# Turning tiles in 32 by 32 blocks on VectorE and placing the blocks by DMA, in an attention and FFN kernel

## The chip, the core and the metric

The kernel runs on one core of one Trainium2 chip. The core has TensorE (PE: matrix products, and transposes as products with an identity), VectorE (DVE), ScalarE (ACT), GpSimd (POOL), and the queue of SyncE (SP), from which most DMAs are issued. Sixteen DMA engines serve all queues. The metric is the time on the device in microseconds (us), the median of several runs.

## The reference

The input is x of 4 batches, 1024 rows and 512 columns, in float32. What is computed:

```python
def attn(x, Wqkv, bqkv, Wo, bo):            # 16 heads of 32
    kqv = (x @ Wqkv + bqkv).reshape(b, s, 3, 16, 32)
    q, k, v = kqv[:, :, 0], kqv[:, :, 1], kqv[:, :, 2]
    scores = jnp.einsum('bsnh,btnh->bnst', k, q) / math.sqrt(32)
    scores = jnp.triu(scores) + -10000.0 * jnp.tril(ones, k=-1)
    a = jax.nn.softmax(scores, axis=2)
    return jnp.einsum('bnkq,bknh->bqnh', a, v).reshape(b, s, 512) @ Wo + bo

def ffn(y, ...):                            # int32 weights, 2048 wide
    W = (wq.astype(float32) - 128) * scale[:, None]     # for gate, up, down
    return (silu(y @ Wg.T) * (y @ Wu.T)) @ Wd.T

x = x + layernorm(attn(layernorm(x)))
x = x + layernorm(ffn(layernorm(x)))
```

Both layer norms ahead of products are of interest here: the normalized rows lie with rows in partitions, and the products need them with columns in partitions, so each tile of 128 rows by 512 columns must be turned. v, which the projection makes with its columns in partitions, must be turned the other way.

## The kernel before

**Attention.** Work goes by batch b (4), by head block hb (4 blocks of 4 heads), and by half g of the 1024 columns. A pair (b, hb) takes 12 periods: 4 for g = 0, then 8 for g = 1, one for each tile c of 128 keys. A period p does, for its tile, the products of scores to be exponentiated (`weights`, L346: PE into PSUM, ACT's exponential at L384, a triangle on POOL at L386), for a later pair the products whose maxima are wanted (`maxima`, L261: PE, then a minimum and a reduction on DVE, L288 and L292), and the products with v of the tile before (`values`, L395). Each period has two halves u. There are 192 periods after 12 that lead in. In this document the position of a period is p modulo 12; a period begins in the trace with the first of four L359 products. In the first periods of g = 1 the sums over keys are made by accumulating DMAs that POOL issues (L434, two of 512 KB a period): these are issued at the start of the periods at positions 6 to 9. The last two pairs of hb and g go without.

**What goes between.** A planner written in Python places the other work (L655 to L860). Three lanes hold projection pieces with a cost and a due period (`in_piece`, `project_out`); four lists hold whole pieces: "rows", "ln", "turn" and "scan". In its first half each period takes at most one whole piece (`fill_whole`, L770); if none was there, it may take a projection piece at this place (`fill`, L756), and at the end of the period more of them. The order is fixed when the kernel is built; every engine runs its own instructions in that order, SP too.

Three things matter here:
- `ln_stage` (L669) is a pipeline over the eight row tiles of a batch: load (L494), statistics (L76, L77, L79, L80), normalize (L86, DVE), turn. `ln_turn` (L505) makes four PE transposes into one PSUM bank, and ACT copies the bank to `xnT` (L515). For batch 0 this runs before the first period; for the others it is spread over the periods of the batch before.
- `turn_v` (L536) turns half of v of a pair: four PE transposes (L543) and an ACT copy (L544) into `vt`, which `values` reads from the pair's first period on.
- `look` (L583) reads all weights once, to see whether a split into two fp32r parts is exact: 48 tiles, three in four periods from period 0 on, each a DMA on SP (L581) and a maximum on DVE at the period's end (L585). Two buffers: after a look the load for the look after next can start.

`store_out` (L572) and `project_out` (L553) make the output rows of the attention and keep them in DRAM (`x2`), through loads and stores on SP.

**FFN.** Eight groups of four row tiles; each group has 16 iterations i of `gate_up` (L966) and `down` (L998), 24 products in an iteration. While a group runs, the next is prepared: rows loaded at i = 5, means at 7, tile k normalized (`layernorm_tile`, L941) at i = 8 + k and turned (`layernorm_turn`, L956) at i = 9 + k: four PE transposes into a bank of the gate and up products (L960), a cast on ACT (L962), a difference on DVE (L964). The first group is prepared during the attention by `ffn_stage` (L618), in the same manner. Weight blocks are loaded and converted by `load_blocks` (L908) in the even iterations of the first group. In the FFN SP's order is left to the scheduler of the framework.

Of the kernel before, what the change touches and what calls it, by code (L numbers as in the profile page):

```python
# [10 lines left out]
F32 = mybir.dt.float32  # L11
F32R = mybir.dt.float32r
BF16 = mybir.dt.bfloat16
I32 = mybir.dt.int32
# [4 lines left out]
P = 128  # L19
# [8 lines left out]
def tile_attn_ffn_sandwich(  # L28
# [15 lines left out]
    nc = tc.nc  # L44
    B, S, H = x.shape
    I = gate_wt.shape[1]
    HC = H // P
    D = 32
    HPB = P // D
    NJ = S // P  # L50
    NT = B * NJ
    IC = I // P
    GT = 4
# [6 lines left out]
    dram = ctx.enter_context(  # L60
        tc.tile_pool(name="between", bufs=1, space=bass.MemoryType.DRAM)
    )
    x2 = dram.tile([B, S, H], F32, tag="x2", name="x2")
    ident = keep.tile([P, P], F32, tag="ident", name="ident")
    make_identity(nc, ident)

# [18 lines left out]
    def normalized(dst, src, mv, i):  # L85
        nc.vector.tensor_scalar(  # L86
            dst, src, mv[:, i, 0:1], mv[:, i, 1:2], ALU.subtract, ALU.mult
        )

    def weight_blocks(k):  # L90

# [7 lines left out]
    with ExitStack() as actx:  # L99
# [9 lines left out]
        e1, e2, e3, p4 = right("a_e1", 1), right("a_e2", 2), right("a_e3", 3), right("a_4", 4)  # L109
        cpool = right("a_w", 1)  # L110
        p1, p2, p3 = right("a_1", 1), right("a_2", 2), right("a_3", 3)
# [80 lines left out]
        for g, t in enumerate(least):  # L192
# [21 lines left out]

        actx.enter_context(
            tc.manual_schedule(
                engines={
# [16 lines left out]
        state = {}  # L236
        later = []

        def beside(shape, name, dtype=F32):

            first = state.get("first", False) and not state.get("last")
            state["first"] = False
            pool, tag = (ps_own, "own") if first else (ps_big, "big")
            return pool.tile(shape, dtype, tag=tag, name=name)
# [253 lines left out]
        def ln_norm(b, j):  # L500
            xn = e2.tile([P, H], F32, tag="xn", name=f"xn_{b}_{j}")
            normalized(xn, state.pop(("xr", b, j)), state.pop(("mv", b, j)), 0)
            state["xn", b, j] = xn

        def ln_turn(b, j):  # L505
            half, i = divmod(j, NJ // 2)
            if i == 0:
                state["xnT", b, half] = pxn.tile(
                    [P, HC, S // 2], F32, tag="xnT", name=f"xnT_{b}_{half}"
                )  # L510
            xn = state.pop(("xn", b, j))
            pt = beside([P, HC, P], f"xt_{b}_{j}")
            for c in range(HC):
                nc.tensor.transpose(pt[:, c, :], xn[:, ts(c, P)], ident)
            nc.scalar.copy(state["xnT", b, half][:, :, ts(i, P)], pt)  # L515
# [20 lines left out]
        def turn_v(b, hb, half):  # L536

            if half == 0:
                state["vt", b, hb] = p2.tile([P, NJ, P], F32, tag="vt", name=f"vt_{b}_{hb}")
            vT = state["v", b, hb]  # L540
            pv = beside([P, 4, P], f"pv_{b}_{hb}_{half}")
            for i in range(4):
                nc.tensor.transpose(pv[:, i, :], vT[:, ts(4 * half + i, P)], ident)  # L543
            nc.scalar.copy(state["vt", b, hb][:, 4 * half : 4 * half + 4, :], pv)  # L544

        def later_v(b, hb):

# [29 lines left out]

        def look_load(n):
            if n < len(blocks):
                state["look", n] = e2.tile([P, 512], I32, tag="look", name=f"look_{n}")  # L580
                nc.sync.dma_start(state["look", n], blocks[n])  # L581

        def look(n):  # L583
# [73 lines left out]
        emitted = {}  # L657
# [7 lines left out]
        def in_piece(b, hb, which, q):  # L665
            project(b, hb, which, q)
            count(("v" if which == 2 else "qk", b, hb))

        def ln_stage(b, j):  # L669

            if j < NJ:
                ln_load(b, j)
            if 0 <= j - 1 < NJ:
                ln_stats(b, j - 1)
            if 0 <= j - 2 < NJ:
                ln_norm(b, j - 2)
            if 0 <= j - 3 < NJ:
                ln_turn(b, j - 3)
            count(("ln", b))

        def normed(b, q):
            return emitted.get(("ln", b), 0) >= NJ // 2 * (q // 2 + 1) + 3

        def turn_piece(b, hb, half):
            turn_v(b, hb, half)
# [4 lines left out]
        NQ = S // 256  # L690
        for b in range(B):
            here, after = at[b, 0, 0], at[b, 0, 0] + n_periods // B
            for j in range(NJ + 3):

                put(whole["ln"], 0, here - 24,
                    lambda p, b=b, j=j, t=here - 46: p >= t and (
                        j - 3 < NJ // 2 or b == 0 or emitted.get(("v", b - 1, HC - 1), 0) >= 2
                    ),
                    ln_stage, b, j)
            for hb in range(HC):  # L700
                i = at[b, hb, 0]
                for q in range(NQ):
                    for which in range(2):

                        put(lanes["qk"], FULL, i - LEAD - 1 + (4 if q >= NQ // 2 else 0),
                            lambda p, b=b, i=i, q=q: p >= i - 24 and normed(b, q),
                            in_piece, b, hb, which, q)

                early = 2 if (b, hb) == (B - 1, HC - 1) else 0
                for q in range(NQ):  # L710
                    put(lanes["v"], FULL, i - 4 - 2 * early,
                        lambda p, b=b, i=i - early, q=q: p >= i - 11 and normed(b, q),
                        in_piece, b, hb, 2, q)
                for half in range(2):
                    put(whole["turn"], 0, i - 2,

                        lambda p, b=b, hb=hb, half=half, n=NQ // 2 * (half + 1):
                            emitted.get(("v", b, hb), 0) >= n
                            and (not half or at[b, hb, 0] == 0
                                 or ("shared", steps[steps.index((b, hb, 0)) - 1]) in emitted),  # L720
                        turn_piece, b, hb, half)
            for j in range(NJ):
                for half in range(2):
                    due = after + 39
                    put(lanes["out"], FULL, min(due, n_periods - 1 if j < 4 else n_periods + 9),
                        lambda p, t=after - 4 + WAIT if j < 4 else after + 4 + WAIT: p >= t,
                        project_out, b, j, half)
            put(lanes["out"], 0.1, due + 1,
                lambda p, b=b: state.get(("rows at", b, NJ - 1), p) < p, store_out, b, NJ - 1)

        def heads(of, p):
            return sorted(
                (lane[0][1], k) for k, lane in of.items() if lane and lane[0][2](p)
            )
# [33 lines left out]
                most -= 1  # L768

        def fill_whole(p):  # L770
            ahead = sorted(heads(whole, p), key=lambda h: h[1] not in ("rows", "scan"))
            if ahead:
                piece(whole[ahead[0][1]])
            return bool(ahead)


        while emitted.get(("ln", 0)) != NJ + 3:
# [20 lines left out]
        for p in range(-LEAD, n_periods + 1):  # L798
# [52 lines left out]
            if p >= 0 and p % 4 != 3:  # L851
                n = next(looks, None)
# [22 lines left out]
    def ffn(exact):  # L875
        MM = F32R if exact else F32
        with ExitStack() as fctx:
# [18 lines left out]
            p2 = pool("f_2", 2)  # L896
            p4 = pool("f_4", 4)
            spool = pool("f_stage", 3)
            e1 = pool("f_e", 1)
            ps_acc = pool("f_acc", 1, space=bass.MemoryType.PSUM)  # L900
            ps_gu = pool("f_gu", 4, space=bass.MemoryType.PSUM)
# [23 lines left out]
            rows, means, xns, normed = {}, {}, {}, {}  # L925
# [15 lines left out]
            def layernorm_tile(t0, i):  # L941
                if i == 0:
                    if exact and t0 // GT % 2 == 0:
                        normed[t0] = [pre["hi"], pre["lo"]]
                    else:
                        normed[t0] = [
                            (p1 if exact else p2).tile(
                                [P, HC, GT * P], MM, tag=f"xnT2{k}", name=f"xnT2{k}_{t0}"
                            )
                            for k in range(1 + exact)  # L950
                        ]
                xn = p2.tile([P, H], F32, tag="xn2", name=f"xn2_{t0 + i}")
                normalized(xn, rows[t0][i], *means[t0 + i])
                xns[t0 + i] = xn

            def layernorm_turn(t0, i):  # L956
                xn = xns.pop(t0 + i)
                pt = ps_gu.tile([P, HC, P], F32, tag="gu", name=f"xt2_{t0 + i}")
                for c in range(HC):
                    nc.tensor.transpose(pt[:, c, :], xn[:, ts(c, P)], ident)  # L960
                parts = [t[:, :, ts(i, P)] for t in normed[t0]]
                nc.scalar.copy(parts[0], pt)  # L962
                if exact:
                    nc.vector.tensor_tensor(parts[1], pt, parts[0], ALU.subtract)  # L964
# [79 lines left out]
            kept = []  # L1044
            for t0 in range(0, NT, GT):
                for i in range(IC):
# [4 lines left out]
                    was, nxt = t0 - GT, t0 + GT  # L1051
# [6 lines left out]
                        load_rows(nxt)  # L1058
                    if nxt < NT and i == 7:
                        layernorm_means(nxt, range(GT))  # L1060
                    if nxt < NT and 0 <= i - 9 < GT:
                        layernorm_turn(nxt, i - 9)
                    if nxt < NT and 0 <= i - 8 < GT:
                        layernorm_tile(nxt, i - 8)
                    if len(kept) > 1 and (nxt < NT or i < IC - 2):
# [65 lines left out]
```

## Time and profile before

| What | us |
|---|---|
| median of 3 runs (range) | 1895.65 (1895.38 to 1896.06) |
| the profiled execution | 1899.55 |
| its span, first to last instruction | 1897.8 |
| PE busy | 1827.5 |
| DVE busy | 1170.4 |
| POOL busy | 720.0 |
| ACT busy | 662.5 |
| four PE transposes of v, from their start to the next product | 0.58 |
| an FFN iteration with a turn, without | 5.94, 5.44 |

The attention with its lead-in takes up to about 1180 us, the FFN the rest. Times in the lines that follow are from the span's start. A line of a group gives line, engine, operation, output and input names, shapes and count, then busy us and mean ns of one, then the idle time of the engine before them and what ended it. A line of a timeline gives start and length. A window line gives, for each engine, busy us and the number of instructions, and at the end the clock granted to TensorE as a share, the busy share of the DMA engines and GB/s. A line of the DMA view gives the packets of a queue, MB, and the share of the 16 engines' time; or a kind of DMA with its count, size and the median us from issue to landing.

### The profile page before, as it was taken

The numbers are of one execution on the slowest core, as the hardware profiler recorded it, in microseconds if no ns is written. First come the engines' busy times: TensorE is split into PE (matmuls) and PEld (weight loads), VectorE is DVE, ScalarE is ACT, GpSimd is POOL, SyncE is SP. The second block draws the span as 40 slices with busy tenths as digits, with TensorE's granted clock in tenths as the row PEclk, the third lists the DMA queues.
The fourth block names the chain that finished last, engine by engine and source line by source line (L and its number), as shares of the span: only waits on it lengthen the run. The fifth ranks groups of instructions, "written<-read, shape, count | busy, mean of one in ns | idle before, by whom it ended". The sixth has DMA issues, their size and how long they took to land. (4 is left out here: it accounts for less than half of the span.)

```text
span 1897.8 us, 40784 instructions
## 1 busy us (share of the span) xinstructions
PE 1827.5 (96%) x17760; PEld 1079.7 (57%) x17761; DVE 1170.4 (62%) x1817; ACT 662.5 (35%) x994; POOL 720.0 (38%) x1000
## 2 busy tenths in 40 slices
PE   7899999999999999999999889999999999999997
PEld 4333444444444444444444335888888888888886
DVE  4688887787776687776667755544444444444344
ACT  2244444444424444424444341222222222222221
POOL 2165555465575465565555653001101010101011
PEclk9999999999999999999999999999999999999999
DMA  3164346435335325424414613501010000101000
GB/s 115 59 145 111 88 110 129 109 78 118 74 80 112 68 63 101 96 63 90 90 37 114 148 68 106 172 34 45 6 40 23 23 17 28 45 1 45 1 23 24
DMA packets 65627, 137.48 MB, mean 72 GB/s; under 512 B 6304, under 2 KB 20640, under 8 KB 65440
## 3 DMA queue, kind: packets, MB, share of 16 engines
q0 software_dynamic: 17280, 62.92, 18.0%
q1 hardware_dynamic: 41008, 67.40, 10.6%
q10 hardware_dynamic: 7152, 4.46, 0.8%
q8 instruction: 141, 2.31, 0.5%
q14 instruction: 46, 0.38, 0.1%
HBM read 55.07 MB, written 16.78 MB: 38 GB/s over the span
## 5 line engine op out<-in xcount | busy, mean ns | idle before, releaser
L292 DVE TENSOR_REDUCE nm<-sc 128x2 f32<-128x1024 f32 (+3 forms) x384 | 366.3, 956 | 119.7 <-PE st L367 103.6
L384 ACT ACTIVATE pT<-st 128x1024 f32<-128x1024 f32 (+3 forms) x384 | 310.4, 811 | 350.3 <-PE st L367 271.6
L252 PE MATMUL pq<-xnT,w 128*32 128x256 f32 x6144 | 369.1, 383 | 5.2 <-ACT xnT L515 2.7
L280 PE MATMUL sc<-in,in 32*128 32x512 f32 (+3 forms) x1536 | 345.9, 535 | 6.1 <-DVE y L563 3.5
L367 PE MATMUL st<-in,in 32*128 32x512 f32 (+3 forms) x1536 | 307.0, 489 | 0.0
L252 PEld LDWEIGHTS pq<-xnT,w 128*32 128x32 f32 x6144 | 186.0, 110 | 182.1 <-issue 25.5
L983 DVE SCALAR_TENSOR_TENSOR h<-pu,pre_us,s 128x512 f32<-128x512 f32 x128 | 96.1, 751 | 310.9 <-PE pu L973 310.3
L1006 PE MATMUL acc<-d,h 128*128 128x512 f32 x896 | 224.8, 393 | 0.2 <-DVE h L993 0.2
L386 POOL TENSOR_SCALAR_AFFINE_SELECT pT<-pT 128x256 f32<-128x256 f32 x256 | 137.0, 545 | 229.2 <-ACT pT L384 229.0
L981 ACT ACTIVATE s<-pg,pre_gs 128x512 f32<-128x512 f32 x128 | 88.1, 689 | 297.2 <-PE pg L973 297.2
L406 PE MATMUL po<-pT,vt 128*32 128x512 f32 (+3 forms) x1536 | 177.7, 501 | 13.2 <-POOL pT L386 12.0
L436 POOL TENSOR_TENSOR pT<-pT,pT 128x768 f32<-128x768 f32 (+1 forms) x120 | 187.0, 1579 | 0.0
L1006 PEld LDWEIGHTS acc<-d,h 128*128 128x128 f32 x896 | 166.1, 188 | 34.3 <-DVE h L993 0.5
L288 DVE TENSOR_TENSOR sc<-sc,bound 128x256 f32<-128x256 f32 x256 | 108.5, 424 | 120.8 <-PE sc L280 77.4
L79 POOL TENSOR_SCALAR rs_y<-mv_y 128x1 f32<-128x1 f32 x32 | 8.8, 275 | 447.7 <-DVE mv_y L77 447.7
L992 ACT CAST h<-h 128x512 fp32r<-128x512 f32 x128 | 79.9, 624 | 248.7 <-DVE h L983 248.7
L434 POOL DMA_DIRECT2D pT<-pT x120 | 106.2, 924 | 99.7 <-DMA pT<-pT 49.6
L993 DVE TENSOR_TENSOR h<-h,h 128x512 fp32r<-128x512 f32 x128 | 88.7, 693 | 88.3 <-ACT h L992 88.3
L359 PE MATMUL st<-mT,ones_bf 3*128 3x512 bf16 (+3 forms) x768 | 125.8, 333 | 15.1 <-ACT pT L384 14.7
L367 PEld LDWEIGHTS st<-in,in 32*128 32x128 f32 x1536 | 134.7, 191 | 0.2
L252 PE MATMUL py<-wo_sb,o 128*32 128x256 f32 x2048 | 124.5, 392 | 9.7 <-DVE pre_lo L628 5.2
L359 PEld LDWEIGHTS <-ones_bf 3*128 3x128 bf16 x768 | 38.1, 91 | 160.3 <-issue 155.6
(133 smaller groups left out, 2625.8 us busy)
## 6 DMA issues: line engine op xcount, KB each, us to landing
pT<-pT POOLq DMA_DIRECT2D x120, 512.0 KB, 5.5
xr<-in_x SPq DMA_DIRECT2D x32, 256.0 KB, 2.9
xo<-in_x SPq DMA_DIRECT2D x32, 256.0 KB, 2.8
x<-xo SPq DMA_DIRECT2D x32, 256.0 KB, 2.0
out<-y SPq DMA_DIRECT2D x32, 256.0 KB, 2.0
look<-in_gate_wt SPq DMA_DIRECT2D x16, 256.0 KB, 2.9
look<-in_up_wt SPq DMA_DIRECT2D x16, 256.0 KB, 2.7
look<-in_down_wt SPq DMA_DIRECT2D x16, 256.0 KB, 3.0
```

What stands on the lines that cost most here:

```text
L252: nc.tensor.matmul(out[k * D : (k + 1) * D, :], lhsT=lhsT[:, k * D : (k + 1) * D], rhs=rhs, start=(c == 0), stop=(c == len(pairs) - 1),)
L280: nc.tensor.matmul(sc[:, h % 2, :n], lhsT=qT[h * D : (h + 1) * D, ts(j, P)], rhs=kT[h * D : (h + 1) * D, 512 * k : 512 * k + n], start=Tru ...
L288: nc.vector.tensor_tensor(sc[:, :, n - P : n], sc[:, :, n - P : n], bound.unsqueeze(1).to_broadcast((P, 2, P)), ALU.min,)
L292: nc.vector.tensor_reduce(nm[:, k, jj, 2 * u : 2 * u + 2], sc[:, :, :n], AX.X, ALU.max, negate=True)
L359: nc.tensor.matmul(st[h // 2][:, h % 2, :n], lhsT=ones_bf[h * D : h * D + 3, :], rhs=mT[h * D : h * D + 3, 512 - n :], start=True, stop=False,
L367: nc.tensor.matmul(st[h // 2][:, h % 2, :n], lhsT=kT[h * D : (h + 1) * D, ts(c, P)], rhs=qT[h * D : (h + 1) * D, q0 : q0 + n], start=False ...
L384: nc.scalar.activation(pT[:, :, :n], st[u][:, :, :n], AF.Exp)
L386: nc.gpsimd.affine_select(out=pT[:, :, :P], in_=pT[:, :, :P], compare_op=ALU.is_ge, fill=0.0, base=0, pattern=[[0, 2], [1, P]], channel_mu ...
L406: nc.tensor.matmul(state["po"][h * D : (h + 1) * D, 512 - n :], lhsT=v[:, c, h * D : (h + 1) * D], rhs=pT[:, h, :n], start=(c == 0), stop= ...
L434: nc.gpsimd.dma_start(total, pT, accum_op=ALU.add)
L436: nc.gpsimd.tensor_tensor(total[:, :, 512 - n :], total[:, :, 512 - n :], pT[:, :, :n], ALU.add)
L1006: nc.tensor.matmul(acc[t0][t], lhsT=part[:, ts(t, P)], rhs=dw[i * P // IB][:, i % (IB // P), :], start=(i == 0 and k == 0), stop=(i == IC ...
```

## The change

- `ln_turn` for batches 1 to 3: no PE transposes and no ACT copy. A normalized tile goes to DRAM (`x1`, one DMA of 256 KB). A stage later `ln_back` loads it (`turned_load`: four DMAs, one for each 32 partitions, in pieces of 32 floats) so that each block of 32 by 32 lies where its transpose belongs, and a further stage later one DVE transpose of the 128 by 512 tile turns every block in place and writes `xnT`. The pipeline is one stage longer (`turn_at`, 4 for these batches). `xb` takes buffers of `xn` (two in all).
- `turn_v`: one DVE transpose of the blocks into `vb` (one buffer), one DMA to DRAM (`v_turned`), four DMAs back into `vt`.
- FFN, groups after the first: the normalized tile is written to DRAM (`x3`) and loaded by `turned_load` right after; `layernorm_turn` comes one iteration later (i = 10 + k) and is one DVE transpose into an SBUF tile, from which the cast and the difference are made as before.
- `look` has one buffer where it had two.
- `fill_whole` now reports that it did something only if a PSUM bank was taken, so after a turn without PE a projection piece may follow at the same place.

Batch 0's rows and the FFN's first group stay with PE.

```diff
+    def turned_load(dst, src):
+        for k in range(4):
+            nc.sync.dma_start(
+                dst[k * 32 : (k + 1) * 32].rearrange("i c (a r) -> i c a r", r=32),
+                src.rearrange("(a i) (c k r) -> k i c a r", i=32, k=4, r=32)[k],
+            )
...
+            state["banks"] = state.get("banks", 0) + 1
...
             state["xn", b, j] = xn
+            if b:
+                nc.sync.dma_start(x1[b, j * P : (j + 1) * P, :], xn)
+
+        def ln_back(b, j):
+            xr = e2.tile([P, H], F32, tag="xn", name=f"xb_{b}_{j}")
+            xr = xr.rearrange("p (c n) -> p c n", c=HC)
+            turned_load(xr, x1[b, j * P : (j + 1) * P, :])
+            state["xb", b, j] = xr
...
             xn = state.pop(("xn", b, j))
+            if b:
+                nc.vector.transpose(
+                    state["xnT", b, half][:, :, ts(i, P)], state.pop(("xb", b, j))
+                )
+                return
...
-            vT = state["v", b, hb]
-            pv = beside([P, 4, P], f"pv_{b}_{hb}_{half}")
-            for i in range(4):
-                nc.tensor.transpose(pv[:, i, :], vT[:, ts(4 * half + i, P)], ident)
-            nc.scalar.copy(state["vt", b, hb][:, 4 * half : 4 * half + 4, :], pv)
+            vt = state["vt", b, hb][:, 4 * half : 4 * half + 4, :]
+            vb = e1.tile([P, 512], F32, tag="vb", name=f"vb_{b}_{hb}_{half}")
+            nc.vector.transpose(vb, state["v", b, hb][:, ts(half, 512)])
+            kept = v_turned[b, hb, half]
+            nc.sync.dma_start(kept, vb)
+            for k in range(4):
+                nc.sync.dma_start(
+                    vt[k * D : (k + 1) * D].rearrange("i c (h d) -> i c h d", d=D),
+                    kept.rearrange("(h i) (c k d) -> k i c h d", i=D, k=4, d=D)[k],
+                )
...
-                state["look", n] = e2.tile([P, 512], I32, tag="look", name=f"look_{n}")
+                state["look", n] = e1.tile([P, 512], I32, tag="look", name=f"look_{n}")
...
-            if 0 <= j - 3 < NJ:
-                ln_turn(b, j - 3)
+            if 0 <= j - turn_at(b) < NJ:
+                ln_turn(b, j - turn_at(b))
+            if b and 0 <= j - 3 < NJ:
+                ln_back(b, j - 3)
...
-            return bool(ahead)
+            return state.get("banks", 0) > banks
...
-                xns[t0 + i] = xn
+                b, j = divmod(t0 + i, NJ)
+                kept = x3[b, j * P : (j + 1) * P, :]
+                nc.sync.dma_start(kept, xn)
+                xr = p2.tile([P, HC, P], F32, tag="xr2", name=f"xr2_{t0 + i}")
+                turned_load(xr, kept)
+                xns[t0 + i] = xr
...
-                xn = xns.pop(t0 + i)
-                pt = ps_gu.tile([P, HC, P], F32, tag="gu", name=f"xt2_{t0 + i}")
-                for c in range(HC):
-                    nc.tensor.transpose(pt[:, c, :], xn[:, ts(c, P)], ident)
+                xr = xns.pop(t0 + i)
+                pt = e1.tile([P, HC, P], F32, tag="pt2", name=f"xt2_{t0 + i}")
+                nc.vector.transpose(pt, xr)
...
-                    if nxt < NT and 0 <= i - 9 < GT:
-                        layernorm_turn(nxt, i - 9)
+                    if nxt < NT and 0 <= i - 10 < GT:
+                        layernorm_turn(nxt, i - 10)
```

## The prediction

> **What bounds the kernel now.** First the page. It gives the span, the busy shares and the chain that ended last.
>
> ```profile
> span 1897.8 us, 40784 instructions
> PE 1827.5 (96%) x17760; PEld 1079.7 (57%) x17761; DVE 1170.4 (62%) x1817; ACT 662.5 (35%) x994; POOL 720.0 (38%) x1000
> PE 36%; DVE 0%; POOL 0%; DMA 0%; issue 0%; ACT 0%; POOLq 0%; DVEq 0%; SPq 0%
> ```
>
> TensorE is busy nearly always, and the chain (it reaches back only through the FFN) is TensorE alone. A turn taken off TensorE is therefore a gain in the FFN at once. In the attention the share hides two kinds of period, so I cut it into windows of one period each (periods and their positions 0 to 11 are explained above). Three of them, at positions 8, 9 and 4; the first columns are length, PE, PEld, DVE, ACT and POOL busy:
>
> ```profile
> 183.90:189.70 5.80, 5.80 (x70) 2.35 (x67) 4.49 (x7) 3.11 (x4) 2.54 (x6) 1.00 1.07 209
> 189.70:194.40 4.70, 4.70 (x64) 1.86 (x60) 4.67 (x6) 2.10 (x3) 3.46 (x5) 1.00 0.80 131
> 284.80:290.20 5.40, 5.02 (x66) 2.08 (x64) 5.26 (x7) 2.53 (x3) 5.40 (x8) 1.00 0.16 51
> ```
>
> At position 8 DVE has 1.3 us to spare; at 9 and 4 it has 0.03 and 0.14. The same cut over all periods gives a mean DVE share of 90, 94 and 89% at positions 0, 4 and 9, and 51 to 76% elsewhere. So DVE binds with PE at 0, 4 and 9, and PE alone elsewhere.
>
> Third, the DMA view. The answers are for 108.5 to 111 us (two queues at once), 172.5 to 198 us (positions 6 to 10) and 198.4 to 226 us (11 to 4):
>
> ```profile
> q0 software_dynamic: 84, 0.34, 83.5%
> q1 hardware_dynamic: 81, 0.17, 19.8%
> ...
> q0 software_dynamic: 1040, 3.74, 81.3%
> ...
> look<-in_up_wt SPq DMA_DIRECT2D x3, 256.0 KB, 4.7
> ...
> look<-in_up_wt SPq DMA_DIRECT2D x4, 256.0 KB, 2.5
> ```
>
> At positions 6 to 9 POOL's accumulating DMAs (q0) fill the sixteen engines, with pauses of about a microsecond. A look load then lands after 4.7 us, else after 2.5. In the first window the two queues move 84 and 81 packets: one of SP's for one of POOL's.
>
> **What is removed.** PE turns: 32 of v, 24 of rows (3 batches of 8), 28 in the FFN.
>
> ```profile
> 261.11 0.66 PE L543 MATMUL pv<-ident,in 128*128 128x128 f32 x4 [0.16 <-ACT in L531]
> 261.69 0.64 PE L406 MATMUL po<-pT,vt 128*32 128x256 f32 x8
> ...
> 1304.69 1.98 PE L1006 MATMUL acc<-d,h 128*128 128x512 f32 x8
> 1310.13 1.98 PE L1006 MATMUL acc<-d,h 128*128 128x512 f32 x8
> 1315.58 0.60 PE L960 MATMUL xt<-ident,xn 128*128 128x128 f32 x4
> 1321.52 0.60 PE L960 MATMUL xt<-ident,xn 128*128 128x128 f32 x4
> ```
>
> A turn holds PE for 261.69 - 261.11 = 0.58 us in the attention. In the FFN an iteration with a turn takes 1321.52 - 1315.58 = 5.94 us, one without 5.44: 0.50 each. FFN: 28 x 0.50 = 14.0 us, all on the path. Attention: of the 32 turns of v, 25 stand in periods that PE binds (2 lie before the first period, 5 at positions 0, 4, 9); of the 24 of rows, 15. 40 x 0.58 = 23.2 us. The 56 ACT copies (L544, L515, 0.59 us each) go too; ACT is at 35%: nothing.
>
> **What is added on DVE.** 84 block turns of 128x512. No row shows one. The nearest is one pass of that size, SBUF to SBUF:
>
> ```profile
> L86 DVE TENSOR_SCALAR xn<-xr,mv_a 128x512 f32<-128x512 f32 x32 | 20.7, 646 | 2.9 <-PE xt L514 2.7
> ```
>
> I take 0.65 us. The Trainium skill (VectorE: DVE Perf Modes, the three transpose paths) has 311 ns for 128x128 in bf16, thus an estimate of 1.24 for four; the same table has TensorE at 390, so a turn on DVE is no bargain. 14 of the attention's 56 stand at positions 0, 4, 9 and lengthen them: 14 x 0.65 = 9.1 us (17.4 by the page; 7.6 at 0.54, the fastest L86 row). I take the row. The rest lies in DVE's slack, which at position 8 is 1.3 us. In the FFN DVE works 2.7 of the 5.94 us of a turning iteration (0.75 + 0.69 + 0.69 + 0.54).
>
> With every DMA in time the sum is 23.2 + 14.0 - 9.1 = 28 us gained.
>
> **What is added on SP.** Each turned tile has one write of 256 KB and four loads of 512 pieces of 128 B: 420 more DMAs, where SP had 235 by the page's issues. An issue costs 0.33 us and back to back 0.6, so four take 2.4. The page's queues price a small packet: q10, 7152 packets at 0.8% of 16 x 1897.8, is 34 ns for 624 B; q1, 41008 at 10.6%, is 78 ns for 1644 B; drawn down to 128 B that is 12 ns. 128 packets per engine then take 1.6 us, hidden under the issues. A load on quiet engines lands 2.4 + 2.2 = 4.6 us after its first issue (bounds 4 and 8, for 7 to 40 ns a packet), the write 2.0 before.
>
> FFN: the turn comes two iterations (11 us) after the normalization; 2.0 + 4.6 fits, with nothing from POOL in flight. In the first group SP also orders weight loads around these. A row load waits for the next tile's write, one iteration on: some 6 us after that against 7.5. Cost 0, at most 3.
>
> Attention, v: the loads are needed 2 to 10 periods later (the tightest, head block 3 of batch 0, has 12 us against 8): no wait on PE. But SP runs in order, and each issue needs one of eight semaphores back from the issue eight before. So what is queued behind v's loads matters.
>
> **Where it stalls.** At positions 6 to 9 the trace's one-for-one turn applies: 81 packets over 16 engines in 2.5 us is one per 0.49 us per engine. 128 small packets would need 60 us; in truth they wait for the pauses. The skill (DMA: Bandwidth & Descriptors, queues, rings and completion order) has an engine drain a whole packet of some 9 to 17 descriptors before it changes rings; then a load has 8 to 14 turns of 0.34 us (q0's packet) and lands after some 8 us. The row shows 2 KB packets only; I take it for 128 B too, as each descriptor there is a packet. Under it:
>
> (a) Rows. xb has in effect one buffer, so its load starts when DVE has turned the tile before, and DVE's next turn is often one period later. Outside 6 to 9 that fits or lacks 0.5 us. Inside it happens at periods 31, 32, 33 (batch 1), 79 and 127: the load, issued about 2 us into the period, gets through some 10 to 13 us later, the turn comes after 6. DVE waits about 7 us in the first of each run (three), 2 in the other two: 25 us. Behind DVE's turn stand the score reductions; two PSUM banks let PE run half a period on: 70%, 17 us.
>
> (b) The look with one buffer. Its load starts only after the reduce before. Issue gaps of 4 to 6 us hold 2.5 us but not always 4.4 to 6.1: about 12 of 48 lack 1 us, half of it felt: 6 us.
>
> (c) Look loads behind v. At periods 20 and 44 the second half's write and loads queue behind the first half's starved ones, and the look load behind both: it lands about 10 us late. At 8 and 56 about 3 late. 26 us, 70%: 18. From period 64 on there are no looks.
>
> (d) Output rows (xo, x2) behind the same loads: 3 us, 0 to 10.
>
> Losses 44, gains 28: +16 on the profiled execution (1899.55 us, span 1897.8, 0.2% over the median). The difference carries over: 1895.65 + 16 = 1912.
>
> **Rivals.** *Grouped packets* (ends on the other side): if the 128 B pieces go in groups, (a) shrinks to 5 waits of 2 us (7 felt), (c) to 4, (b) and (d) to 4: 15 lost, 28 gained, 1883; with hardly any wait, 1870. The point that decides is a load's landing in positions 6 to 9: below 8 us it is faster. For it: the queue pauses, and PE idles when DVE does, so POOL's next DMAs come later too. Against it: the 84 to 81.
> *Slow pieces*: if a piece costs 40 ns even on quiet engines, a load takes 8 us, and every turn one period after its load (11 of 24) waits 2 to 3 us more, and looks 8 in all: 35 more, 1947. For it: no row has strided 128 B reads. Against it: 512 B cost under 34 ns.
> *Cancelling*: the change does what it says and half the waits come: within 4 us of before.
>
> **Chances.** Starved loads 0.50 (own range 1899 to 1932), slow pieces 0.15, grouped 0.29, cancelling 0.06. 0.2% (3.8 us) is about what a measurement of this kernel tells from no change: slower 0.65, same 0.06, faster 0.29. The range 1872 to 1955 leaves out the best tenth (no wait at all) and the worst.
>
> **What would show it.** L514 down to the first batch, L543 and L960 gone; a block turn near 0.65 us; FFN iterations all at 5.44. Right: DVE's block turn and look reduce wait for DMAs for tens of us, mostly at 240 to 270 us and where periods 79 and 127 lie; landings of xb and vt over 10 us at positions 6 to 9, under 5 else. Wrong: landings below 8 us everywhere, or a turn over 1.2 us.

## The result, and the profile after

| | before | changed |
|---|---|---|
| median of 4 runs each, us (range) | 1895.86 (1895.38 to 1897.31) | 1922.17 (1920.42 to 1926.10) |
| ratio to before, 95% interval | | 1.0134 (1.0111 to 1.0157) |
| the profiled execution, its span, us | 1899.55, 1897.8 | 1920.74, 1918.6 |
| mean granted TensorE clock | 0.992 | 0.977 |

The change made the kernel 26.3 us slower by the medians, 21.2 by the two profiled executions; the forecast was 1912, +16. First the page of the changed kernel: span, engines, queues, and the chain that ended last.

```profile
span 1918.6 us, 40822 instructions
PE 1801.0 (94%) x17423; PEld 1054.6 (55%) x17425; DVE 1224.5 (64%) x1901; ACT 632.0 (33%) x938; POOL 709.4 (37%) x1000
...
q1 hardware_dynamic: 230512, 111.47, 21.5%
q0 software_dynamic: 17280, 62.92, 17.9%
...
PE 77%; DVE 8%; DMA 5%; POOL 5%; ACT 2%; issue 2%; SPq 1%; DVEq 0%; POOLq 0%; ACTq 0%
...
L458 POOL DMA_DIRECT2D pT<-pT x120 | 105.9, 913 | 114.9 <-DMA pT<-pT 67.9
...
pT<-pT POOLq DMA_DIRECT2D x120, 512.0 KB, 6.4
...
v_turned<-vb SPq DMA_DIRECT2D x32, 256.0 KB, 3.9
vt<-v_turned SPq DMA_DIRECT2D x128, 64.0 KB, 3.4
```

PE is busy for 26.5 us less, and yet the span is 21 longer. The chain now passes through DVE, DMA and POOL as well; that of before was PE alone, but it reached back only through the FFN. The FFN did what was wanted. PE's timeline of the changed kernel, around three iterations that prepare tiles for the next group:

```profile
1346.98 1.98 PE L1060 MATMUL acc<-d,h 128*128 128x512 f32 x8
1352.42 1.98 PE L1060 MATMUL acc<-d,h 128*128 128x512 f32 x8
1357.86 1.98 PE L1060 MATMUL acc<-d,h 128*128 128x512 f32 x8
```

Every iteration takes 5.44 us, where those with a turn took 5.94. The time from the start of the last period to the end of the span is 732.6 us, before 745.8: 13.2 less. The lead-in up to the first period is 4.3 us shorter (71.6 against 75.9). All that was lost, was lost in between. One window over the time from the first period to the last, before and then changed (length, PE, PEld, DVE, ACT and POOL busy, then the granted clock, DMA share and GB/s):

```profile
75.94:1152.06 1076.12, 1034.15 (x13436) 450.63 (x13434) 799.80 (x1180) 462.29 (x676) 620.36 (x831) 0.99 0.42 93
```

```profile
71.59:1186.02 1114.43, 1025.07 (x13220) 437.43 (x13219) 832.86 (x1234) 429.97 (x622) 610.01 (x831) 0.96 0.54 116
```

The stretch is 38.3 us longer. PE's idle time in it (length less PE busy) rose from 42.0 to 89.4 us, by 47.4, while its busy time fell by only 9.1 us. Some 54 turns of 0.58 us (all but the two of v in the lead-in) would be 31.3. The missing 22 us are in the clock column, as shown below.

**Where PE stood idle.** The longest wait, at 197 to 205 us. The changed kernel's timeline of SP, then of DVE and PE (start, length; in brackets the engine's idle time before it and what ended it):

```profile
177.84 0.33 SPq L624 DMA_DIRECT2D look<-in_gate_wt  x1
180.91 0.33 SPq L582 DMA_DIRECT2D v_turned<-vb  x1
186.87 3.69 SPq L584 DMA_DIRECT2D vt<-v_turned  x4
190.60 1.04 SPq L582 DMA_DIRECT2D v_turned<-vb  x1
197.06 2.60 SPq L584 DMA_DIRECT2D vt<-v_turned  x4
199.76 4.53 SPq L624 DMA_DIRECT2D look<-in_up_wt  x2
...
203.24 0.69 DVE L628 TENSOR_REDUCE greatest<-look 128x1 f32<-128x512 int32 x1 [7.81 <-DMA look<-in_up_wt]
203.84 0.42 DVE L312 TENSOR_TENSOR sc<-sc,bound 128x256 f32<-128x256 f32 x1
204.29 0.69 DVE L316 TENSOR_REDUCE nm<-sc 128x2 f32<-128x512 f32 x1
...
205.04 0.80 PE L304 MATMUL sc<-in,in 32*128 32x128 f32 x4 [7.28 <-DVE nm L316]
```

SP stands at the first load of v until the write before it has landed: 180.91 to 186.87, and 190.60 to 197.06 for the second half. A write that lands in 2.0 us on quiet engines takes some 6 here. The look's load, next on SP, goes out at 199.76. DVE has stood at that look for 7.81 us. Behind it in DVE's order are the minimum and the maxima of scores, and PE waits for those, 7.28 us. The look loads themselves are hardly slower. From issue to landing they take about what they took before (this one 3.5 us; the median of its kind was 2.7 before). The changed kernel's DMA view of the whole span:

```profile
look<-in_up_wt SPq DMA_DIRECT2D x16, 256.0 KB, 2.9
```

They are issued late.

**What the waiting DVE costs in all.** The changed kernel's groups of instructions on `greatest` (what the looks write), and those on `xb` (the rows as loaded back):

```profile
L628 DVE TENSOR_REDUCE greatest<-look x48: 621/676/689, 76.9 to 444.0; 128x1 f32<-128x512 int32 x48
...
its engine sat idle before it (us, times) until:
  DMA look<-in_down_wt: 17.1, 6
  DMA look<-in_up_wt: 12.2, 4
  DMA look<-in_gate_wt: 4.0, 3
```

```profile
L545 DVE STREAM_TRANSPOSE xnT<-xb x24: 651/703/711, 141.9 to 838.3; 128x512 f32<-128x512 f32 x24
its engine sat idle before it (us, times) until:
  DMA xb<-x: 14.9, 4
```

33.3 us at looks and 14.9 at the turned rows, 48.2 together. Before the change DVE waited for no look.

**Why the transfers are late.** The changed kernel's DMA view of 189 to 190 us and of 190 to 192.5:

```profile
q0 software_dynamic: 48, 0.20, 121.1%
q1 hardware_dynamic: 48, 0.01, 8.1%
```

```profile
q0 software_dynamic: 78, 0.25, 60.9%
q1 hardware_dynamic: 1519, 0.19, 51.1%
```

While POOL's accumulating DMAs fill the engines, SP's 128 B pieces pass one for one with packets of some 4 KB: 48 to 48, 0.01 MB beside 0.20. By the starts of the packets these are three rounds of sixteen, each small piece with a large packet a few ns behind it. When POOL's queue runs dry within the second window, 1519 of SP's packets pass.

**The clock.** After PE has stood idle, it is slow for a while. Windows of the changed kernel around the wait above (the column after POOL's is the granted clock):

```profile
186.90:197.30 10.40, 10.40 (x154) 4.44 (x148) 8.42 (x11) 5.18 (x8) 6.16 (x11) 1.00 1.10 209
197.30:200.40 3.10, 0.47 (x10) 0.27 (x6) 0.00 (x0) 0.38 (x1) 0.00 (x0) 0.89 0.64 110
200.40:206.20 5.80, 1.16 (x9) 0.71 (x13) 2.90 (x7) 0.00 (x0) 0.30 (x1) 0.50 0.37 106
206.20:210.60 4.40, 4.40 (x50) 1.87 (x42) 3.39 (x8) 0.86 (x2) 4.32 (x5) 0.57 0.52 148
```

The clock is 0.50 from 199.7 to 210.0 us. PE works again at 205 and is at half rate for 5 us more. Added up from the first period to the last, such stretches make 78.5 us (20.5 before), each a multiple of about 3.4 us. PE was busy in them for 62.4 us, before for 19.2; at full rate half of the difference, 21.6 us, would not have been needed. With it the sum closes: 47.4 (idle) + 21.6 (half rate) - 31.3 (turns) = 37.7, measured 38.3. The Trainium skill (TensorE: Matmul & The Clock Gate, Part 1: The HAM clock gate) has the clock at half after an idle window of some 3.4 us and back at full after a busy one; the lengths of the stretches agree with it. The idle times do not all: two of 1.47 and 0.81 us close together (from 134.65 us) brought half rate at 138.3 us, and of the ten over 2 us in this stretch nine were followed by it; one of 2.95 us (from 847.04 us) was not.

### The profile page after: what moved, and what is told of

It reads as the page before. It is cut to its first block, busy times and chain, and to the rows that moved or that the text cites. A ratio compares the mean times of both kernels' runs of the same rounds, so it can differ in the third digit from the quotient of the medians.

```text
span 1918.6 us, 40822 instructions
## 1 busy us (share of the span) xinstructions
PE 1801.0 (94%) x17423; PEld 1054.6 (55%) x17425; DVE 1224.5 (64%) x1901; ACT 632.0 (33%) x938; POOL 709.4 (37%) x1000
## 3 DMA queue, kind: packets, MB, share of 16 engines
q0 software_dynamic: 17280, 62.92, 17.9%
## 4 chain that ended last, share of the span: by engine, by line
PE 77%; DVE 8%; DMA 5%; POOL 5%; ACT 2%; issue 2%; SPq 1%; DVEq 0%; POOLq 0%; ACTq 0%
PE pq L276 15%; PE pg L1027 12%; PE pu L1027 12%; PE acc L1060 12%; PE sc L304 8%; PE po L430 5%; PE st L383 4%; PE py L276 3%; PE st L391 2%; PE pd L441 2%; DVE nm L316 2%; ACT pT L408 2%; DMA pT<-pT 2%; POOL pT L460 2%; DMA xb<-x 1%
## 5 line engine op out<-in xcount | busy, mean ns | idle before, releaser
L276 PE MATMUL pq<-xnT,w 128*32 128x256 f32 x6144 | 377.6, 389 | 4.4 <-ACT xnT L552 2.7
L304 PE MATMUL sc<-in,in 32*128 32x512 f32 (+3 forms) x1536 | 351.4, 543 | 27.6 <-DVE nm L316 27.4
L410 POOL TENSOR_SCALAR_AFFINE_SELECT pT<-pT 128x256 f32<-128x256 f32 x256 | 126.0, 500 | 226.3 <-ACT pT L408 226.1
L276 PE MATMUL py<-wo_sb,o 128*32 128x256 f32 x2048 | 130.9, 403 | 23.6 <-DVE y L606 19.5
L458 POOL DMA_DIRECT2D pT<-pT x120 | 105.9, 913 | 114.9 <-DMA pT<-pT 67.9
L304 PEld LDWEIGHTS sc<-in,in 32*128 32x128 f32 x1536 | 116.2, 188 | 39.4 <-DVE nm L316 30.0
```

The lines of the kernel that those rows point to most:

```text
L276: nc.tensor.matmul(out[k * D : (k + 1) * D, :], lhsT=lhsT[:, k * D : (k + 1) * D], rhs=rhs, start=(c == 0), stop=(c == len(pairs) - 1),)
L304: nc.tensor.matmul(sc[:, h % 2, :n], lhsT=qT[h * D : (h + 1) * D, ts(j, P)], rhs=kT[h * D : (h + 1) * D, 512 * k : 512 * k + n], start=Tru ...
L410: nc.gpsimd.affine_select(out=pT[:, :, :P], in_=pT[:, :, :P], compare_op=ALU.is_ge, fill=0.0, base=0, pattern=[[0, 2], [1, P]], channel_mu ...
```

## The experiments

My theory: SP's transfers for v and the rows are starved beside the accumulating DMAs; DVE then waits, at looks because their loads stand behind v's, and at `xb` directly. The rival after the result: the new transfers slow POOL's accumulating DMAs, too (the wait for them in POOL's row above is 67.9 us, before 49.6), and the loss comes through POOL and ACT. Each result stands with the kernel before as run beside it, whose median moved from 1895.86 to 1897.69 between groups of runs. A difference to the changed kernel is one of medians; by the ratios those across groups are some 1 to 2 us larger.

**No accumulating DMAs.** In both kernels the 120 accumulating DMAs are left out; the sums over keys then lack these parts.

```diff
-                if wide:
-                    nc.gpsimd.dma_start(total, pT, accum_op=ALU.add)
-                else:
+                if not wide:
```

> The kernel before without the accumulating DMAs of POOL (the sums over keys of the first five tiles of a half are left out, so the softmax is divided by a wrong sum). It is the base for the next run. POOL loses 120 issues of 0.9 us, PE none: 1885 to 1895 us.

> The changed kernel without the accumulating DMAs of POOL (the same sums left out as in the run before it). Theory (the small pieces starve beside the accumulates): with those gone every turned load lands within 6 us, DVE's waits for DMAs fall below 10 us, and the change is worth its 20 to 30 us: that much faster than the kernel before without them. Rival (SP's order and its waits for writes cost by themselves, or DVE's work does): it stays 10 us or more slower than that kernel.

Measured: 1889.12 us for the kernel before so cut (0.9952 of before, 0.9934 to 0.9971), 1869.63 for the changed one (0.9852, 0.9832 to 0.9871). The change now gains 19.5 us instead of losing 26. In the changed kernel without the accumulates, the DMA view shows landings as on quiet engines:

```profile
v_turned<-vb SPq DMA_DIRECT2D x32, 256.0 KB, 2.0
vt<-v_turned SPq DMA_DIRECT2D x128, 64.0 KB, 2.6
...
xb<-x SPq DMA_DIRECT2D x96, 64.0 KB, 2.6
```

DVE waits 7.4 us at looks and 0.4 at `xb`. So the two together, small pieces and accumulates, make the loss; this does not yet say which of them waits for the other.

**One part at a time.** v back to PE; rows back to PE; and both, with the looks in two buffers again (the FFN part alone):

```diff
-            vb = e1.tile([P, 512], F32, tag="vb", ...)
-            nc.vector.transpose(vb, state["v", b, hb][:, ts(half, 512)])
...
+            pv = beside([P, 4, P], f"pv_{b}_{hb}_{half}")
+            for i in range(4):
+                nc.tensor.transpose(pv[:, i, :], vT[:, ts(4 * half + i, P)], ident)
+            nc.scalar.copy(state["vt", b, hb][:, 4 * half : 4 * half + 4, :], pv)
```

> The changed kernel with v turned by PE and ACT as before; rows and FFN as in the change, the look still with one buffer. Theory: with v's loads gone from SP the looks wait little, which gives back about 35 us of idle PE and half clock; lost are v's savings of some 15 us on PE: about 1902 us, clock about 0.985. Rival (DVE's added work costs): 5 block turns at positions 0, 4 and 9 less, 3 us better, less v's 15 us of saving: 1934.

Measured: 1898.49 us (1897.69 before; ratio 1.0001, 0.9992 to 1.0010). v costs the changed kernel 23.7 us. DVE's waits at looks fall to 5.3 us without it, those at `xb` to 8.9.

```diff
         def turn_at(b):
-            return 4 if b else 3
+            return 3
```

(`ln_turn` and `ln_norm` as before the change.)

> The changed kernel with the rows of batches 1 to 3 turned by PE and ACT as before; v and FFN as in the change. Theory: PE's idle times at periods 33, 70 and 119 (13 us) and the half clock after each go, some 20 us, against 3 us net that these rows saved: about 1905 us; the looks' waits behind v at periods 22 and 46 stay. Rival (DVE's added work): 9 block turns of 0.7 us less: 6 us better, less 9 us of savings: 1925.

Measured: 1907.69 us (1.0045, 1.0031 to 1.0059). The rows cost the changed kernel 14.5 us. The look waits remain, 35.0 us, and make this the kernel to mend in the next experiments.

> Only the FFN's part of the change: rows and v of the attention by PE, the look with two buffers. Theory: 28 turns of 0.50 us leave PE and nothing waits: 1896 - 13 to 14 = 1882 to 1883 us. Rival (the FFN's gain in the changed kernel is a shift of the boundary): less than 8 us.

Measured: 1880.55 us (1897.34 before; 0.9905, 0.9882 to 0.9927). The FFN part gains 16.8 us, somewhat more than its 14.0. In the trace 13.0 of it lie in the FFN. Of the rest, periods 176 to 179 are shorter than in the kernel before, by 6.9 us in the traces; the only edit of this kernel that reaches them is what `fill_whole` reports. That edit was not run alone. Against this kernel the one with the rows but without v (1898.49) is 17.9 us slower, so the rows lose without v as well. DVE's waits there are the 8.9 us at `xb` and 5.3 at looks; no run takes these apart.

**The look's buffer.** The kernel before, with one buffer for the look:

```diff
-                state["look", n] = e2.tile([P, 512], I32, tag="look", name=f"look_{n}")
+                state["look", n] = e1.tile([P, 512], I32, tag="look", name=f"look_{n}")
```

> The kernel before with one change alone: the look has one buffer instead of two. Theory (starved loads): DVE waits for look loads about 6 us in all where the accumulating DMAs run, none of the long waits of 5 to 8 us, since nothing stands ahead of the look on SP; half of it is felt: 1896 + 3 to 6 = about 1900 us. Rival (the single buffer itself is what costs): the 7 to 8 us waits at periods 22 and 46 are here too and the time is 1910 or more. Granted clock as before, 0.99.

Measured: 1897.70 us (1897.69 before; 0.9999, 0.9990 to 1.0007). One buffer costs nothing by itself, though DVE waits 5.4 us at eight looks where it waited at none.

**The looks on another queue.** In the changed kernel, the look loads are issued on ACT's queue, one period after they were:

```diff
-                nc.sync.dma_start(state["look", n], blocks[n])
+                nc.scalar.dma_start(state["look", n], blocks[n])
...
-            look_load(n + 1)
+            state["want"] = n + 1
...
                     weights(*now, [u] if unit else range(2))
+                if "want" in state:
+                    look_load(state.pop("want"))
```

> The changed kernel, but the look loads are issued from ACT's queue, early in the period after the reduce, so they stand neither behind the loads of v on SP nor behind their packets in the ring. Theory: the looks' waits on DVE fall from 33 us to under 10, PE's idle times at periods 23, 47, 39 and 59 go with the half clock that follows them, and the time falls from 1922 to about 1890 to 1897. Rival (DVE's added work at positions 0, 4 and 9 is what costs, the waits are absorbed): no more than 3 us better, 1919.

Measured: 1912.64 us (1.0078, 1.0056 to 1.0101): 9.5 better than the changed kernel, a third of what was expected. DVE still waits 16.4 us at looks. The same with the rows by PE:

> v and the FFN as in the change, the rows of batches 1 to 3 by PE, the look loads from ACT's queue. Theory: both kinds of long wait are gone, the savings of v (about 11 us net) and of the FFN (13 to 14) stay: about 1872 us, faster than both kernels. Rival (v's block turns on DVE and its DMAs give nothing even without waits): 1883, as the FFN alone.

Measured: 1894.79 us (1897.34 before; 0.9983, 0.9974 to 0.9992), 12.9 better than with the look on SP, where 1872 was expected. Look waits are 19.6 us. From ACT's queue a load waits for its place in ACT's order, and then beside other queues, up to 7.9 us to landing. I took this miss for a sign that slowed accumulates carry the rest: ACT's exponentials waited 16.5 and 18.5 us for accumulating DMAs in these two, 4.6 before. The sign was weak: the FFN part alone, without small pieces in the attention, has 11.3. The next runs tell the two apart.

**Earlier looks, and no looks.** With the rows by PE: the look's load issued two looks ahead, on SP.

```diff
-                state["look", n] = e1.tile([P, 512], I32, tag="look", name=f"look_{n}")
+                state["look", n] = e2.tile([P, 512], I32, tag="look", name=f"look_{n}")
...
-            look_load(n + 1)
+            look_load(n + 2)
```

(A second load is issued at the start, and `vb` takes buffers of `xn`, to make room.)

> The changed kernel with the normalized rows turned by TensorE (as in the run with rows by PE, 1907.69 us), v and the FFN's later groups by VectorE, and the looks in two buffers, each load issued two looks ahead instead of one; still on SP's queue. Theory (v's starved pieces make the look loads behind them late): a look load has some 5 us more, DVE's waits at looks (7.9, 6.6, 7.8 and 4.1 us there, 31 in all) fall below 8 us in all, and the time to 1886 (1907.7 less 16 of PE's felt waits and less the half-clock time after them). Rival (the delay is elsewhere: v's pieces slow the accumulating DMAs and ACT and POOL wait for those, as the run with looks on ACT's queue suggested): the looks' waits go, but the time stays at 1897 or above.

Measured: 1885.51 us (1897.44 before; 0.9927, 0.9902 to 0.9951), where 1886 was expected: 22.2 better than with the looks one ahead. DVE's waits at looks, in this kernel's view of `greatest`:

```profile
  DMA look<-in_up_wt: 5.9, 1
  DMA look<-in_down_wt: 4.5, 2
```

10.4 us in place of 35.0. The edit does two things: it gives the look back its second buffer, and it issues each load earlier in SP's order. From the issue of a load to its look there were 13.7 us at the median in the kernel before, 4.8 in the kernel before with one buffer, 4.9 with the rows by PE, and 15.0 here. So v's transfers did their harm in a lead that the single buffer had shortened; which of the two edits mends it was not run apart, nor was the change of `vb`. The kernel is no faster than the FFN part alone (1880.55).

And with the looks left out altogether (the kernel then takes the exact path without having read the weights' maxima), with and without v on DVE:

> As the run with rows by PE, but the 48 looks at the FFN's weights (loads and reduces) are left out, their maxima set to zero. To be read only against the next run. Theory (looks carry v's loss): v then gains, some 8 us faster than the next run (25 turns of 0.58 us less 5 of 0.7). Rival (slowed accumulates carry it): 6 us or more slower than the next run.

> The FFN part alone, v and rows turned by TensorE, with the 48 looks left out in the same way. Expected 1870 to 1881 us (the FFN part alone took 1880.55; 48 reduces of about half a microsecond less on DVE, of which a third or less was felt).

Measured: 1869.50 us (1868.74 to 1870.11) with v on DVE, 1877.96 (1875.67 to 1879.25) without. With nothing behind v's transfers, v on DVE gains 8.5 us; 8 was expected. POOL's row in the kernel with v on DVE and no looks, after that of the kernel before the change:

```profile
L434 POOL DMA_DIRECT2D pT<-pT x120 | 106.2, 924 | 99.7 <-DMA pT<-pT 49.6
...
L458 POOL DMA_DIRECT2D pT<-pT x120 | 106.1, 923 | 102.6 <-DMA pT<-pT 68.6
```

POOL waits as long for its DMAs as in the changed kernel (67.9; 52.1 without v and looks), and ACT's exponentials 22.5 us, longer than in the two runs on ACT's queue. And yet v gains. So the slowed accumulates are there, but they don't carry v's loss: the rival falls for v. v loses through the looks behind it on SP. For the rows no such run was made.

**A version to keep.** The FFN part, and v on DVE in batches 2 and 3 only, after the last look:

```diff
+            if b >= 2:
+                vt = state["vt", b, hb][:, 4 * half : 4 * half + 4, :]
+                vb = e2.tile([P, 512], F32, tag="xn", name=f"vb_{b}_{hb}_{half}")
...
+                return
             vT = state["v", b, hb]
```

> The FFN part, and v by VectorE in batches 2 and 3 only, where no looks stand behind it; rows by TensorE, looks in two buffers. Theory (v loses only through the looks): 16 turns less on PE, 12 of them felt, 7 us, less some 2 for DVE: 1876 us against 1880.55 for the FFN part alone. Rival (v's pieces cost elsewhere too): 1881 or more; for it speaks that with rows by PE the periods from 96 on were 7.4 us shorter than before, with the FFN part alone 8.4.

Measured: 1878.33 us (0.9890, 0.9867 to 0.9913), no waits at looks. That is 1.1% faster than the kernel before. Against the FFN part alone (0.9905, 0.9882 to 0.9927) it isn't told apart: the intervals overlap.

## Why the prediction was right, and where it was off

The direction and the mechanism held; the size was 10 us short by the medians. Of those, 5 come from setting the sum against profiled executions: the profiled one of before was 3.7 us above its median, the changed one 1.4 below. Against the profiled executions it is +16 forecast, +21.2 measured. By its own steps:

| Step | forecast | measured |
|---|---|---|
| FFN turns removed | -14.0 | -13.2 (FFN part of the trace) |
| attention turns, felt, less DVE's block turns | -14.1 | not separable; a block turn took 0.70, not 0.65 |
| DVE's waits at looks, (b) 12 and (c) 26 | 38 | 33.3 |
| DVE's waits at rows, (a) | 25 | 14.9 |
| losses from the first to the last period, net of gains | +30 (44 - 14.1) | +38.3 |
| lead-in | 0 | -4.3 |
| half clock after idling | not in the sum | 21.6 |

- *The pieces.* 12 ns for one of 128 B was estimated from two queues' rows; the packets' median in the trace is 13.0. In the FFN, with nothing of POOL's in flight, turned loads land 4.3 to 6.1 us after their first issue, where 4.6 was forecast. Slow pieces fall.
- *The starvation.* One for one with POOL's packets, taken from rows of 2 KB, holds for 128 B as well (48 to 48 above). Loads issued at positions 6 to 9 landed 5.4 to 11.1 us after their first issue; 10 to 13 was too long. The grouped rival falls, and with it, for these pieces, the figure of the Trainium skill (DMA: Bandwidth & Descriptors, Queues, rings and completion order) that an engine drains a packet of typically some 9 to 17 descriptors of a ring before it changes to the next: here it changed after one piece.
- *(c), the looks behind v.* Where and how as said: 7.81 us at 203 us and 7.59 at 349, where v of periods 20 and 44 stood ahead, and less at the other two (1.88 us at period 11, 2.38 at 59); 5.22 us at period 54 was not foreseen. What was not seen is that the write is starved as well as the loads, and that SP stands still until it lands: 6 us of the wait, twice.
- *(b), one buffer,* was wrong as a cost of its own: alone it made waits of 5.4 us where 12 were forecast, and none was felt. What it does is shorten the lead that (c) needs (4.8 us in place of 13.7). The waits of both came at thirteen looks rather than at twelve and four more places; that 33.3 us came near the 38 of the sum is luck, by an error on each side.
- *(a), the rows.* Waits of 5.64 and 3.57 us at 257 to 272 us, as forecast. Periods 79 and 127 had none; 2.89 and 2.83 came at periods 70 and 119, at the end of a starved stretch. 14.9 in place of 25.
- *(d), output rows:* no cost is seen. POOL's additions on `xo` waited for DVE alone (62.5 us, before 66.5), never for a DMA, and DVE waited for them 7.6 us, before 10.1.
- *The share felt,* 70%, was taken from the PSUM banks, with PE at full rate when it resumes. That is the step that failed: the half clock stood at nothing in the sum. As an estimate, if DVE's turns at positions 0, 4 and 9 made 17.2 us of PE's new idle time as forecast (9.1, and 8.1 of PE turns removed there), the 48.2 us of DVE's waits made the other 30 of the 47.4, or 63%. But each long one brought 3.4 to 10.2 us at half clock behind it, and the added half clock cost 21.6 us in all. With the looks two ahead the time fell by 22.2 us for 24.6 us less of waits, 90%.
- *Two gains unforeseen:* the lead-in, 1.5 to 4.3 us shorter than before in the kernels that turn v of batch 0 on DVE there (the others differ from it by 1.0 us at most), where the forecast had counted only periods; and periods 176 to 179.

The smaller waits and the half clock partly cancelled: waits felt 30 rather than 44, then 21.6 for the clock. That the sum came within 5 us of the profiled executions is in part luck.

## What to carry to other kernels

Before a tile is turned through many small DMAs, look for what else fills the DMA engines at that time, and for what stands behind these DMAs on their queue: v, the larger loss (23.7 us), lost through an unrelated load issued after its transfers, and the rows, the smaller (14.5 us), came with waits for their own transfers (14.9 us). Move such loads ahead (two looks ahead, with a second buffer, gave back 22 us), or keep the small pieces out of the stretches that a large-packet queue fills. And charge a wait that stops PE at more than its length, for the clock it comes back to: here 47.4 us of new idle time came with 21.6 us lost at half clock.

## What the runs showed of the hardware

- Pieces of 128 B on SP's queue alternate one for one with POOL's packets of some 4 KB: 48 and 48 in a microsecond. Without POOL's beside them, as in the FFN, each takes 13.0 ns of an engine at the median, beside them 27.
- After most idle times of PE of 2.0 to 7.3 us, and some shorter ones, the granted clock is 0.50, for 3.4, 6.8 or 10.2 us; in all 78.5 us from the first period to the last of the changed kernel, before 20.5.
- The small pieces slow the large ones in turn: an accumulating DMA of 512 KB landed after 6.4 us at the median, before 5.5; POOL waited 67.9 us for them, before 49.6. In the runs without looks v gained 8.5 us all the same.
- A DVE transpose of 32 by 32 blocks over 128x512 in float32 took 0.70 us, against the estimate of 1.24 from the bf16 128x128 figure of the Trainium skill (VectorE: DVE Perf Modes, The three transpose paths).
